# A sparse GNN and expert kernel on one core: one tile more gathered in quarter rows, the order of its gathers, and the queue of one weight load

## The chip, the cores and the metric

The kernel runs on one core of a Trainium2 chip. The metric is the device time of one execution in microseconds; the number to compare is the median over runs. Three runs of the kernel before gave 282.81, 284.5 and 288.1 us, so its median is 284.5 us.

## The reference

There are 625 rows of 1024 numbers. A first part (a relational graph layer over 20,000 edges) makes a new x; a second part adds a mixture of experts to it. The change lies in the second part, which is this:

```
xf = layernorm(x)                                   # 625 x 1024
sh = gelu(xf @ sW1[s] + sb1[s])                      # 2 shared experts, hidden 256
shared = mean over s of (sh @ sW2[s] + sb2[s])
gates = xf @ rW + rb;  w = softmax of the top 2 of 8 # per row
h = gelu(xf @ W1[e] + b1[e]);  y = h @ W2[e] + b2[e] # 8 experts, 1024 -> 256 -> 1024
out = x + shared + sum over e of w[e] * y[e]
```

All tensors are 32-bit floats. The kernel computes an expert only for the rows that chose it.

## The kernel before, in words

The first 119 us are the graph layer. Its last step writes the normalised rows to a DRAM tensor `h2d`, from which rows are gathered later. Then TensorE computes the first layer of the two shared experts (`p_sh`, line 1146, eight products of 128 by 512 in two column cuts for each of four blocks). In its shadow VectorE finds, for every row, the two best experts (`route`), and packs the rows into 11 tiles of 128 slots (`slots`): seven tiles (4 to 10) belong to one expert each, three (0, 1, 2) to two experts with 64 slots each, one (3) to four experts with 32 slots each. `tok` holds the row number of each slot of each tile. `quarter_rows` (line 1420) makes from it `tok4`: four row numbers for each slot, for a gather in which each partition gets quarters of four different rows, so that a transpose in blocks of 32 by 32 on VectorE gives the tile with columns on the partitions. For this TensorE multiplies four 128 by 128 selectors (`own4`, line 1424) with `tf`, a copy of `tok`, and VectorE scales the result into `tok4` (line 1431). `weights_T` (line 1400) splits the routing weights into three bfloat16 parts and transposes them; they are needed by the last products `p_o`.

`quarter_rows` is called from inside `shared_in(1, 0)`, between its two column cuts, by the argument `then` (line 1245). The instructions of each engine are put in order by the framework from the program's order and the waits written out as `tc.issue_after`.

Then comes the stage around the change, the first layer of the experts. It goes over the 11 tiles in the order

```
whole = range(NM2, NJ)
tiles = (*whole[:3], 0, whole[3], 1, whole[4], 2, *whole[5:], NH2)   # 4 5 6 0 7 1 8 2 9 10 3
by_quarters = [tiles[i] for i in (0, 1, 3, 5, 7, 9)]                 # 4 5 0 1 2 10
```

For each tile:

- `gather` (line 1465): GpSimd (POOL) issues indirect DMAs from `h2d` into the tile's rows `xs`, which have three buffers. A tile in `by_quarters` takes four, one for each quarter (line 1468); any other takes one of whole rows (line 1473).
- `fetch` (line 1477): a tile in `by_quarters` is turned by one VectorE transpose into `xsT` (line 1485). For any other, TensorE transposes the rows (`turn`, line 1496, two bursts `p_x` of four 128 by 128 transposes); ScalarE evicts the first burst (line 1502), VectorE the second (line 1500). The two first tiles are turned into the place of the second weights of expert 7 (`w2a[:, 7]`), which is free until those are loaded.
- `copy_w1` (line 1504): where a tile has several experts, ScalarE copies the weights of its second and further experts into `w1m` (line 1509).
- `expert_in` (line 1511): TensorE multiplies with the first weights (`p_h`, line 1515), VectorE copies the product to `hj` (line 1519), which has a single buffer, and SP's queue stores it in DRAM (`hd`, line 1521). Four more DMAs of SP's queue (`to_quarters`, line 1528) read the tile before this one back in another order as `hjT`.
- `expert_mid` (line 1534): VectorE transposes `hjT` in 32 by 32 blocks into `hT` (line 1537) and ScalarE applies bias and gelu (line 1542).

The second weights of experts 0 to 6 are loaded on SP's queue before the routing (`load_w2`, line 1182). Those of expert 7 are loaded on the same queue in step 2 of the loop over the tiles, when the products of tiles 4 and 5 have read what stood in their place.

Behind this stage TensorE computes the second layer (`p_yj`, line 1578), whose rows are scattered to DRAM (`yt`) and read back by row (`g`, line 1636), and the second layer of the shared experts (`p_o`, line 1676); VectorE adds all to x and the rows are stored.

Of the kernel before, what the change touches and what calls it, by code (L numbers as in the profile page):

```python
# [12 lines left out]
I32 = mybir.dt.int32  # L13
# [11 lines left out]
NE = 8  # L25
# [428 lines left out]
def sparse_kernel(  # L454
# [24 lines left out]
    nc = tc.nc  # L479

    def pool(stack, name, bufs=1, side="left", **kw):
        return stack.enter_context(tc.tile_pool(name=name, bufs=bufs, side=side,
                                                reuse_waits="tile", **kw))

    const = pool(ctx, "const")
# [10 lines left out]
    def ps_acc(name):  # L496
        return psum[0].tile([128, 512], F32, tag="acc", name=name, bufs=nacc[0])

    def ps_mm(name):
        return psum[0].tile([128, 512], F32, tag="mm", name=name, bufs=3)  # L500
# [146 lines left out]
    def bias_part(i):  # L647
        own = slice(0, (3 - i) * QC)
        near = b23.rearrange("p (k d) -> p k d", k=KD)
        if i:  # L650
# [14 lines left out]
                                    ap=[[0, 4], [D, QC], [1, D]]))  # L665
# [386 lines left out]
    turned = []  # L1052
# [90 lines left out]
    def shared_products(p, i, t, c, ks):  # L1143
        a, z = CUTS[c]
        for k in ks:
            nc.tensor.matmul(p[:, : z - a], sw1[:, i, k, t * 128 : (t + 1) * 128],  # L1146
                             h2T[:, k, a:z], start=(k == 0), stop=(k == KD - 1))
# [30 lines left out]
    io = pool(ctx, "io", 3)  # L1178
    w2a = pool(ctx, "w2a").tile([128, NE, HK, D], F32, name="w2a")

    def load_w2(e):
        nc.sync.dma_start(w2a[:, e], W2[e].rearrange("(k p) d -> p k d", p=128))

    for e in range(NE - 1):
        load_w2(e)
# [56 lines left out]

    shT = hid.tile([128, NS, HK, N], F32, name="shT")

    def shared_in(i, t, then=lambda: None):
        b = KD + i * HK + t
        for c, (a, z) in enumerate(CUTS):
            if a:
                then()
            first = not (i or t or c)  # L1250
            p = begun if first else ps_acc(f"p_sh_{i}_{t}_{a}")
            shared_products(p, i, t, c, range(AHEAD if first else 0, KD))
            nc.scalar.activation(shT[:, i, t, a:z], p[:, : z - a], AF.Gelu, bias=vT[:, b : b + 1])
# [5 lines left out]
    wab = const.tile([TP, 2, NT], F32, name="wab")  # L1259
    tok = const.tile([128, NJ], I32, name="tok")  # L1260
    tok4 = const.tile([128, 4, NJ], I32, name="tok4")
    quad = const.tile([128, 1], F32, name="quad")
    for b in range(4):
        nc.gpsimd.memset(quad[b * QC : (b + 1) * QC], float(b))
# [135 lines left out]
    def weights_T():  # L1400
        nc.vector.tensor_scalar(w[:, :, NS:], w[:, :, NS:], float(NS), None, op0=ALU.mult)
        NW_ = NS + NE
        part = rt.tile([TP, NT, 3 * QC], F32, name="part")
        nc.vector.memset(part, 0.0)
        near = const.tile([TP, NT, NW_], BF16, name="near")
        for i in range(3):
            nc.vector.tensor_copy(near, w)
            for j in range(3):
                at = j * QC + i * NW_
                nc.vector.tensor_copy(part[:, :, at : at + NW_], near)  # L1410
            if i < 2:
                nc.vector.tensor_sub(w, w, near)
        for a, b in ((0, 3), (3, NT)):
            p = ps_mm(f"p_wT_{a}")
            for d in range(a, b):
                nc.tensor.transpose(p[: 3 * QC, (d - a) * TP : (d - a + 1) * TP], part[:, d, :],
                                    ident[:TP, :TP])
            nc.vector.tensor_copy(wT[:, a * TP : b * TP], p[: 3 * QC, : (b - a) * TP])

    def quarter_rows():  # L1420
        own4 = rt.tile([128, 4, 4, QC], F16, tag="above", name="own4")
        tf = rt.tile([128, NJ], F16, name="tf")
        for a in range(4):
            nc.scalar.copy(own4[:, a], ident[:, None, a * QC : (a + 1) * QC].to_broadcast([128, 4, QC]))
        with tc.issue_after(named.ins):
            nc.vector.tensor_copy(tf, tok)
        q4 = ps_mm("p_tok4")
        for a in range(4):
            nc.tensor.matmul(q4[:, a * NJ : (a + 1) * NJ], own4[:, a].rearrange("p b r -> p (b r)"), tf,
                             start=True, stop=True)  # L1430
        return nc.vector.tensor_scalar(tok4.rearrange("p a j -> p (a j)"), q4[:, : 4 * NJ], 4.0, quad,
                                op0=ALU.mult, op1=ALU.add)

    gate()
    route()
    named = slots()
    weights_T()
    turned = []
    shared_in(1, 0, lambda: turned.append(quarter_rows()))
    shared_in(1, 1)  # L1440
    sh_in.close()

# [10 lines left out]
    def parts(j):  # L1453
        if j < NH2:
            return (0, HS, e_of[j]), (HS, 128, e_of[NH2 + j])
        if j < NM2:
            return [(QS * i, QS * (i + 1), e_of[nt + i]) for i in range(4)]
        return ((0, 128, e_of[NH2 + j - 1]),)

    xsT, w1m, copied, moved = {}, {}, [], []  # L1460
    acts = []
# [3 lines left out]
    def gather(j):  # L1465
        if j in by_quarters:
            for a in range(4):
                nc.gpsimd.indirect_dma_start(  # L1468
                    out=rows[j][:, a * (D // 4) : (a + 1) * (D // 4)], out_offset=None,
                    in_=h2d.rearrange("n (b f) -> (n b) f", b=4),  # L1470
                    in_offset=bass.IndirectOffsetOnAxis(ap=tok4[:, a, j : j + 1], axis=0))
        else:
            nc.gpsimd.indirect_dma_start(
                out=rows[j], out_offset=None, in_=h2d,
                in_offset=bass.IndirectOffsetOnAxis(ap=tok[:, j : j + 1], axis=0))
# [17 lines left out]
    def turn(j, g):  # L1493
        p = ps_acc(f"p_x{g}_{j}")
        for k in range(4):
            nc.tensor.transpose(p[:, k * 128 : (k + 1) * 128], half_row[j][:, 4 * g + k :: KD], ident)  # L1496
        o = xsT[j][:, 4 * g : 4 * g + 4, :]
        pv = p.rearrange("p (k n) -> p k n", k=4)
        if g:
            turned.append(nc.vector.tensor_copy(o, pv))  # L1500
        else:
            acts.append(nc.scalar.copy(o, pv))
# [8 lines left out]
    def expert_in(j):  # L1511
        p = ps_mm(f"p_h_{j}")
        for k in range(KD):
            for a, b, e in parts(j):
                nc.tensor.matmul(p[a:b, :H], xsT[j][:, k, a:b],  # L1515
                                 w1m[j, a][:, 0, k, :] if a else w1a[:, bass.ds(e, 1), k, :],
                                 start=(k == 0), stop=(k == KD - 1))
        h = xt.tile([128, H], F32, tag="hj", bufs=1, name=f"hj_{j}")
        copied.append(nc.vector.tensor_copy(h.rearrange("p (q c r) -> p c q r", q=4, c=HK),  # L1519
                                           p[:, :H].rearrange("p (c q r) -> p c q r", c=HK, q=4)))  # L1520
        moved.append(nc.sync.dma_start(hd[j], h))
        if j not in (tiles[0], tiles[-1]):
            with tc.issue_after(moved[-1].ins):
                to_quarters(tiles[tiles.index(j) - 1])

    def to_quarters(j):
        for q in range(4):
            nc.sync.dma_start(hjT[32 * q : 32 * q + 32, j].rearrange("t c (b r) -> t (c b r)", b=4)
                              .rearrange("t (b x) -> t b x", b=4),
                              hd[j].rearrange("(b t) (q x) -> q t b x", b=4, q=4)[q])  # L1530
# [15 lines left out]

    whole = range(NM2, NJ)
    tiles = (*whole[:3], 0, whole[3], 1, whole[4], 2, *whole[5:], NH2)
    by_quarters = [tiles[i] for i in (0, 1, 3, 5, 7, 9)]
    copies = {}  # L1550
    for i, (j, a, e) in zip((2, 3, 5, 6, 8, 9), ((j, a, e) for j in tiles for a, _, e in parts(j)[1:])):
        copies[tiles[i]] = [(j, a, e)]
    for i in (1, 0, 2):
        rows[tiles[i]] = io.tile([128, D], F32, tag="io", name=f"xs_{tiles[i]}")
    for i in (2, 0, 1):
        gather(tiles[i])
    for s in range(NJ + 2):
        if 0 < s <= NJ and tiles[s - 1] in half_row:
            turn(tiles[s - 1], 1)
        if s < NJ:  # L1560
            if s > 2:
                rows[tiles[s]] = io.tile([128, D], F32, tag="io", name=f"xs_{tiles[s]}")
                gather(tiles[s])
            fetch(tiles[s])
        if 0 <= s - 1 < NJ:
            expert_in(tiles[s - 1])
        if s == 2:
            load_w2(NE - 1)
        if 0 <= s - 4 < NJ - 3:
            expert_mid(tiles[s - 4])  # L1570
    ORDER = (*whole[:3], *range(NM2), *whole[3:])
# [38 lines left out]
    for n, j in enumerate(ORDER):  # L1610
        y = gat.tile([128, D], F32, tag="y", name=f"ys_{j}")
        for s in range(2):
# [3 lines left out]
            p = p_ys[j, s]  # L1616
# [47 lines left out]
    for d in range(NT):  # L1664
# [3 lines left out]
        for at in ((0, 512), (512, D)) if d < NT - 1 else ((0, 512), (512, 768), (768, D)):  # L1668
            n = at[1] - at[0]
            at = slice(*at)  # L1670
            p = (ps_mm if banks % 8 > 4 else ps_acc)(f"p_o_{d}_{at.start}")
# [21 lines left out]
def gnn_ffn_kernel(tc, *args):  # L1693
    nc = tc.nc
    with tc.tile_pool(name="flags", bufs=1) as flags:
        flag = flags.tile([1, 1], I32, name="flag")
        off = sparse_kernel(tc, flag, *args)
        with tc.If(off > 0):
            dense_kernel(tc, *args)
# [31 lines left out]
```

## Time and profile before

The profiled execution took 285.32 us, its span is 283.5 us, and the granted TensorE clock was 0.997 of full speed.

| | us | share of the span | instructions |
|---|---|---|---|
| TensorE matmul (PE) | 274.4 | 97% | 1509 |
| TensorE weight load (PEld) | 183.3 | 65% | 1509 |
| VectorE (DVE) | 175.7 | 62% | 446 |
| ScalarE (ACT) | 101.8 | 36% | 232 |
| GpSimd (POOL) | 61.1 | 22% | 122 |

The transfers sum to 64.48 MB, 227 GB/s over the span. SP's queue carries 48.74 MB of them, GpSimd's 15.04 MB, ScalarE's 0.35 MB.

How to read it: a line of a timeline is the start in us from the start of the span, the length, the engine, the line of the kernel, the operation, the tile that it writes and those it reads, and the number of instructions merged; in square brackets stands how long the engine was idle before it and what ended that. "SPq" is SP's queue of DMAs; the length is that of the issue, not of the transfer. Tile names are printed without their numbers. The chain that ended last is followed back from the last instruction: at each step to what released it, or to the instruction before it on its engine. Products are merged there, so that x16 is one tile's product with 128 slots (each 32-bit product counts as two instructions).

### The profile page before, as it was taken

The page shows a single profiled execution, that of the slowest core. Times are in us where ns is not written, and L with a number is a line of the kernel's source. Part 1 is how long each engine was busy: PE and PEld are TensorE (multiplying, and loading weights), DVE is VectorE, ACT ScalarE, POOL GpSimd, SP SyncE. Part 2 cuts the span into 40 slices and gives each one's busy share as a digit, 9 for nine tenths or more (in the row PEclk, how much of TensorE's full clock was granted, in tenths as well). Part 3 has the DMA queues.
Part 4 walks back from the last instruction along what each step waited for, and adds up shares of the span by engine and source line. Part 5 has one row for each costly group of instructions (what it writes and reads, how often), then busy time and mean ns, then how long its engine had stood idle before and what let it go on. Part 6 is the DMA issues. An engine that isn't in the chain of part 4 may idle for free.

```text
span 283.5 us, 4565 instructions
## 1 busy us (share of the span) xinstructions
PE 274.4 (97%) x1509; PEld 183.3 (65%) x1509; DVE 175.7 (62%) x446; ACT 101.8 (36%) x232; POOL 61.1 (22%) x122
## 2 busy tenths in 40 slices
PE   8899999999999999999999999799999999999993
PEld 7667777788888655677777787678544324444452
DVE  4889999999975689838930641555341312216972
ACT  2347326534642242445101150856298311100000
POOL 9810020000000032210047555360020222210000
PEclk9999999999999999999999999999999999999998
DMA  7999981000000899998999279754296554439962
GB/s 226 356 324 355 371 289 47 2 0 2 1 0 2 322 369 425 420 375 321 390 415 393 88 221 283 202 154 137 68 329 217 218 205 191 186 115 385 392 219 79
DMA packets 29987, 64.48 MB, mean 227 GB/s; under 512 B 8961, under 2 KB 16196, under 8 KB 28935
## 3 DMA queue, kind: packets, MB, share of 16 engines
q1 hardware_dynamic: 24475, 48.74, 47.9%
q0 software_dynamic: 5200, 15.04, 15.1%
q10 hardware_dynamic: 284, 0.35, 0.4%
q8 instruction: 14, 0.23, 0.3%
q14 instruction: 14, 0.11, 0.1%
HBM read 44.63 MB, written 20.26 MB: 229 GB/s over the span
## 4 chain that ended last, share of the span: by engine, by line
PE 82%; DMA 8%; DVE 7%; SPq 1%; issue 0%; ACT 0%; DVEq 0%
PE p_pr L956 15%; PE p_yj L1578 14%; PE p_o L1676 12%; PE p_sh L1146 12%; PE p_h L1515 10%; PE p_y L1031 6%; PE p_agg L985 5%; DMA xh<-in_x_dram 4%; DMA hd<-hj 4%; DVE st L777 2%; PE cnt L934 2%; PE p_t L844 2%; DVE ohs L903 1%; PE p_x L1496 1%; PE p_gate L1198 1%; PE p_y L1032 1%
## 5 line engine op out<-in xcount | busy, mean ns | idle before, releaser
L956 PE MATMUL p_pr<-wg,nT 128*125 128x286 f32 x240 | 62.4, 410 | 0.9 <-DVE neg L798 0.6
L956 PEld LDWEIGHTS p_pr<-wg,nT 128*125 128x125 f32 x240 | 43.3, 187 | 13.4 <-ACT nT L850 1.2
L1578 PE MATMUL p_yj<-w2a,hjT 128*128 (+2 forms) x88 | 38.7, 595 | 0.0
L1676 PE MATMUL p_o<-sw,shT 128*125 128x512 f32 (+1 forms) x88 | 36.3, 553 | 0.0
L1146 PE MATMUL p_sh<-h2T,sw 128*128 128x313 f32 (+1 forms) x128 | 35.3, 429 | 0.0
L1515 PE MATMUL p_h<-w1a,xsT 128*128 (+2 forms) x144 | 32.7, 380 | 1.5 <-DVE xsT L1485 1.5
L1578 PEld LDWEIGHTS p_yj<-w2a,hjT 128*128 128x128 f32 (+2 forms) x88 | 14.5, 168 | 23.3 <-issue 22.8
L1146 PEld LDWEIGHTS p_sh<-h2T,sw 128*128 128x128 f32 x128 | 23.6, 189 | 8.5 <-issue 0.2
L1515 PEld LDWEIGHTS p_h<-w1a,xsT 128*128 128x128 f32 (+2 forms) x144 | 22.8, 163 | 7.7 <-issue 1.7
L1676 PEld LDWEIGHTS p_o<-sw,shT 128*125 128x125 f32 x88 | 16.4, 187 | 16.9 <-issue 15.9
L1468 POOL DMA_INDIRECT xs<-h2d,tok x24 | 22.7, 946 | 19.0 <-issue 5.8
L1618 DVE COPY ys<-p_yj 128x512 f32<-128x512 f32 x15 | 10.3, 689 | 26.1 <-PE p_yj L1578 26.1
L1625 POOL DMA_INDIRECT yt<-ys,row x11 | 10.7, 970 | 48.9 <-DVE ys L1618 48.9
L1519 DVE COPY hj<-p_h 128x256 f32<-128x256 f32 x11 | 4.6, 421 | 24.5 <-PE p_h L1515 19.0
L1031 PE MATMUL p_y<-wo_t,eT 128*125 128x512 f32 (+1 forms) x40 | 18.8, 592 | 0.0
L1042 POOL DMA_DIRECT2D x1d<-xh x4 | 2.2, 542 | 65.6 <-DVE flagf L727 62.1
L1542 ACT ACTIVATE hjT<-hT,vT 128x128 f32<-128x128 f32 (+2 forms) x34 | 9.8, 354 | 17.1 <-DVE hT L1537 10.2
L985 PE MATMUL p_agg<-P,CT 125*125 125x288 f32 x100 | 15.5, 305 | 0.0
L1515 PE MATMUL p_h<-w1m,xsT 128*64 128x256 f32 (+1 forms) x96 | 14.7, 381 | 0.0
L1647 DVE SCALAR_TENSOR_TENSOR x<-g,wab,x 125x1024 f32<-125x1024 f32 (+1 forms) x12 | 13.2, 1105 | 1.9 <-DMA g<-yt 1.7
L1578 PE MATMUL p_yj<-w2m,hjT 128*64 128x512 f32 (+1 forms) x48 | 14.1, 595 | 0.0
L904 DVE TENSOR_TENSOR ohs<-ohs,cols 125x1024 f16<-125x1024 f16 (+1 forms) x22 | 14.0, 638 | 0.0
(306 smaller groups left out, 415.7 us busy)
## 6 DMA issues: line engine op xcount, KB each, us to landing
w1a<-in_L_ffn_W_dram SPq DMA_DIRECT2D x8, 1024.0 KB
w2a<-in_L_ffn_W_dram SPq DMA_DIRECT2D x8, 1024.0 KB
yt<-zero SPq DMA_DIRECT2D x2, 2560.0 KB
g<-yt SPq DMA_DIRECT2D x10, 512.0 KB
sw<-in_L_ffn_sW_dram SPq DMA_DIRECT2D x4, 1024.0 KB
h2d<-h POOLq DMA_DIRECT2D x5, 448.0 KB, 9.5
out_dram<-x SPq DMA_DIRECT2D x4, 448.0 KB
x<-x1d SPq DMA_DIRECT2D x1, 1500.0 KB
```

The source lines that it names most:

```text
L904: last = nc.vector.tensor_tensor(os, os, both(VV_, 128)[1], op=ALU.mult)
L956: product = nc.tensor.matmul(p[:TP, :F], nT[:, k, m * TP : (m + 1) * TP], wg[:, k, r, :], start=(k == 0), stop=(k == KD - 1))
L985: nc.tensor.matmul(p[:TP, : F + 2], CT[:, m, at : at + TP], P[:, m, r, i], start=(m == 0 and i == 0), stop=(m == NT - 1 and i == 1))
L1031: nc.tensor.matmul(ps[s][:TP, :], eT[:n, k, :], wo_t[:n, k, at], start=(k == 0), stop=False)
L1146: nc.tensor.matmul(p[:, : z - a], sw1[:, i, k, t * 128 : (t + 1) * 128], h2T[:, k, a:z], start=(k == 0), stop=(k == KD - 1))
L1468: nc.gpsimd.indirect_dma_start(out=rows[j][:, a * (D // 4) : (a + 1) * (D // 4)], out_offset=None, in_=h2d.rearrange("n (b f) -> (n b) f", ...
L1515: nc.tensor.matmul(p[a:b, :H], xsT[j][:, k, a:b], w1m[j, a][:, 0, k, :] if a else w1a[:, bass.ds(e, 1), k, :], start=(k == 0), stop=(k == ...
L1578: made = nc.tensor.matmul(p[a:b], hjT[:, j, k, a:b], (w2m[j, a, k] if a else w2a[:, bass.ds(e, 1), k])[..., s * 512 : (s + 1) * 512], star ...
L1618: copied.append(nc.vector.tensor_copy(y[:, at], p))
L1625: sent.append(nc.gpsimd.indirect_dma_start(out=yt, out_offset=bass.IndirectOffsetOnAxis(ap=row[:, j : j + 1], axis=0), in_=y, in_offset=No ...
L1647: added.append(nc.vector.scalar_tensor_tensor(*args, op0=ALU.mult, op1=ALU.add))
L1676: nc.tensor.matmul(p[:TP, :n], shT[:, i, k, own], sw2[:, i, k, at], start=(i == 0 and k == 0), stop=False)
```

## The change

Five edits belong together:

1. `quarter_rows` is called right after `slots`, ahead of `weights_T`, and no longer from inside `shared_in`.
2. The tiles in quarter rows are those at places 0, 1, 3, 4, 6, 8 and 10 of the order (4, 5, 0, 7, 8, 9, 3) in place of 0, 1, 3, 5, 7 and 9 (4, 5, 0, 1, 2, 10). TensorE turns 6, 1, 2 and 10 in place of 6, 7, 8, 9 and 3.
3. Four tiles, not three, have their rows allotted and their gathers issued ahead of the loop. On POOL's own list of instructions the gathers of the fourth tile (0) keep their place, their buffer and their wait.
4. The fifth tile (7) takes its four row numbers from `tok5`, a copy of 128 by 4 numbers that VectorE makes right behind the copy of tile 4's product.
5. The second weights of expert 7 are loaded by ScalarE's queue. On ScalarE's list the load stands behind six copies of `w1m` and ahead of two more.

```diff
-    def load_w2(e):
-        nc.sync.dma_start(w2a[:, e], W2[e].rearrange("(k p) d -> p k d", p=128))
+    def load_w2(e, eng=nc.sync):
+        eng.dma_start(w2a[:, e], W2[e].rearrange("(k p) d -> p k d", p=128))
...
-    def shared_in(i, t, then=lambda: None):
+    def shared_in(i, t):
...
-            if a:
-                then()
...
+    tok5 = const.tile([128, 4], I32, name="tok5")
...
     named = slots()
+    turned = [quarter_rows()]
     weights_T()
-    turned = []
-    shared_in(1, 0, lambda: turned.append(quarter_rows()))
+    shared_in(1, 0)
     shared_in(1, 1)
...
-                    in_offset=bass.IndirectOffsetOnAxis(ap=tok4[:, a, j : j + 1], axis=0))
+                    in_offset=bass.IndirectOffsetOnAxis(
+                        ap=tok5[:, a : a + 1] if j == tiles[4] else tok4[:, a, j : j + 1], axis=0))
...
+        if j == tiles[0]:
+            with tc.issue_after(copied[-1].ins):
+                nc.vector.tensor_copy(tok5, tok4[:, :, tiles[4]])
         moved.append(nc.sync.dma_start(hd[j], h))
...
-    by_quarters = [tiles[i] for i in (0, 1, 3, 5, 7, 9)]
+    by_quarters = [tiles[i] for i in (0, 1, 3, 4, 6, 8, 10)]
...
-    for i in (1, 0, 2):
+    for i in (1, 0, 2, 3):
         rows[tiles[i]] = io.tile([128, D], F32, tag="io", name=f"xs_{tiles[i]}")
-    for i in (2, 0, 1):
+    for i in (2, 0, 1, 3):
         gather(tiles[i])
...
-            if s > 2:
+            if s > 3:
...
         if s == 2:
-            load_w2(NE - 1)
+            with tc.issue_after(acts[-1].ins):
+                load_w2(NE - 1, nc.scalar)
```

## The prediction

> **What bounds the kernel now.** I read the page first (busy shares), then the chain that ended last, then busy time by stretch, then the timelines of the stretch that the change touches (145 to 205 us).
>
> ```profile
> span 283.5 us, 4565 instructions
> ...
> PE   8899999999999999999999999799999999999993
> ```
>
> TensorE is busy nearly throughout; one slice outside the first and last is a 7. The table of busy time by stretch says how little idle there is (columns: stretch, its length, then busy us of each engine, clock, DMA share, GB/s):
>
> ```profile
> 166.00:180.00 14.00, 12.49 (x82) 9.98 (x81) 7.08 (x9) 3.96 (x9) 8.51 (x9) 1.00 0.87 258
> 180.00:204.00 24.00, 24.00 (x197) 18.51 (x198) 10.18 (x18) 13.12 (x33) 5.67 (x6) 1.00 0.49 141
> 204.00:248.00 44.00, 44.00 (x151) 17.36 (x151) 11.72 (x20) 19.60 (x35) 9.71 (x10) 1.00 0.59 218
> ```
>
> From 32 us to the last product near 279 us TensorE idles only in 166 to 180, for 14.00 - 12.49 = 1.51 us. So inside the touched part the end moves only through (a) TensorE work removed, (b) that hole, (c) new holes. The chain shows what made the hole (start, length, what):
>
> ```profile
> 166.00 0.44 DVE hj L1519
> 166.46 6.23 DMA hd<-hj
> 172.81 0.44 DVE hj L1519
> 173.26 3.74 DMA hd<-hj
> 177.25 0.09 issue
> 177.46 0.42 DVE hT L1537
> 177.87 1.95 DVE xsT L1485
> 179.82 0.14 issue
> 179.95 3.67 PE p_h L1515 x32
> 183.63 0.64 PE p_x L1496 x4
> 184.27 3.46 PE p_h L1515 x16
> 187.73 0.44 PE p_x L1496 x4
> 188.17 3.60 PE p_h L1515 x32
> ```
>
> The tile hj has one buffer, so VectorE may not copy the next tile's product until the DMA of the last one to DRAM (hd) has landed. VectorE is in order: the transpose xsT of tile 1 stands behind two such copies and ends at 179.8; TensorE, free at 178.4, starts at 179.95. The first of those DMAs took 6.23 us, the second 3.74. Just ahead of the slow one on SP's queue stands one megabyte of second weights (w2a, expert 7); the timeline of SP's queue:
>
> ```profile
> 162.55 0.35 SPq L1521 DMA_DIRECT2D hd<-hj  x1
> 165.99 0.38 SPq L1182 DMA_DIRECT2D w2a<-in_L_ffn_W_dram  x1
> 166.46 0.42 SPq L1521 DMA_DIRECT2D hd<-hj  x1
> ```
>
> **The change, part by part.** Tiles run in the order 4, 5, 6, 0, 7, 1, 8, 2, 9, 10, 3. Before, TensorE turns 6, 7, 8, 9, 3; after, 6, 1, 2, 10. All other tiles are gathered in quarter rows and turned by VectorE.
>
> *One tile less turned by TensorE.* It loses two bursts of four transposes. In the chain a burst takes 0.44 us after a whole tile and 0.64 after a tile of two halves; three bursts still follow such a tile, so the two lost are the cheap ones: 2 x 0.44 = 0.88 us, on the path. ScalarE loses one eviction (0.59), VectorE one (0.69) and gains one transpose (2.03): +1.34 us for VectorE, in a stretch (166 to 180) where it is busy 7.08 of 14. POOL goes from 6 x 4 + 5 = 29 gathers to 7 x 4 + 4 = 32: three more at 0.95 + 0.30 = 1.25 us, 3.75 us of issue. POOL is busy 8.51 of those 14 us, and its last gather before starts at 189.55, for a tile turned from 199.4 on: covered there, provided that the gathers near 170 are in time (below).
>
> *quarter_rows ahead of weights_T.* The same instructions. In the changed order TensorE makes the row numbers after three products of the shared expert instead of after eight and the wT transposes. From 140.70 at 2.74/5 = 0.55 us a product that is 142.3; the input tf is ready at 141.76 and own4 at 130.8, so no wait. VectorE's tok4 ends near 143 instead of 146.0; the last three copies of part (0.43 us) slip behind it to about 143.5, and TensorE reaches wT at 142.6 + 2 x 0.55 = 143.7: nothing. POOL can start the eight quarter gathers at 143.8, behind the whole-row gather that ends at 143.49, not at 146.28. DMA share is 1.02 or more until 156 (seven weight loads), so their data come at most 2.5 us sooner, and TensorE is in p_sh until 158.37 anyhow: worth nothing on the path. It lets the gathers of tile 0 begin near 156 instead of 158.54.
>
> *Fourth gather emitted ahead.* Tile 0's gathers stand in the same place in POOL's order, wait for the same buffer and the same transpose: nothing.
>
> *Fifth held back.* tok5 is a 128x4 copy on VectorE right behind hj of tile 4; the nearest row, a 128x11 cast, takes 0.17 us, and VectorE then waits 3.47 us anyhow. Tile 7's gathers cannot start before 162.52 + 0.17 + 0.30, about 163.0; a whole-row gather of tile 7 started at 163.54 before. Now there are four, to 163.0 + 4 x 1.25 - 0.3 = 167.7, and behind them on POOL the whole rows of tile 1 (167.9 to 168.9; 166.67 to 171.4 before, in quarters), then tile 8. TensorE needs them as follows. Tile 6's product starts at 166.24, tile 0's near 169.70 and ends near 173.30; tile 1's first burst is then due, and tile 7's product at 173.94. VectorE needs 2.03 + 0.14 for tile 7's transpose, so its rows must have landed, and VectorE be free, by 171.8. Gathers take 2.7/3.3/7.8 us to land (minimum, median, maximum of the trace): from 167.7 that is 170.4, 171.0 or 175.5; tile 1's rows, from 168.9, at 171.6, 172.2 or 176.7, against 173.30. At the median both are in time; at the maximum the holes are 3.7 and 3.4 us (they overlap). I take the median, since the 7.8 belongs with the weight loads at full DMA share, and keep 3.7 for the range.
>
> *Expert 7's second weights on ScalarE's queue.* Both orders want tile 5's product done (166.0). On ScalarE the issue stands behind six w1m copies, 163.03 + 6 x 0.53 = 166.2, so it waits for nothing; at 0.38 us like SP's it delays only the two w1m copies behind it, used at 177.8, and the next eviction (173.9). SP loses the issue and its 3 us of waiting. What matters is the landing of tile 5's hd, issued at 166.45 as before, beside the megabyte instead of behind it. Bounds: 6.23 us if sharing the engines is as bad as queueing, 3.74 (the next hd; the one of 162.55 needed at most 3.45) if it is as if alone. I take 4.2, near the low end, because hd moves an eighth of the bytes. Then hj of tile 6 starts at 170.7 and ends at 171.1, and tile 7's transpose is done at 173.1: no hole. At 6.23 it ends at 175.3 and the hole is 1.5 again. Further on: hj of tile 0 must wait for the hd issued at 171.2 and hj of tile 7 for that of tile 0. At 3.74 each, hj of tile 7 starts at 179.1, and the eviction of tile 1's second burst behind it ends at 180.6, while TensorE wants it at the middle of tile 1's product, 177.84 + 1.8 = 179.6: a hole of 1.0. At 2.2 (the hd of 177.55 let hj go at 179.73) there is none. I take 0.3.
>
> [...]
>
> **Sum.** -0.88 (transposes) - 1.51 (hole) + 0.3 (what is left of it) = -2.1 us. Behind 180 TensorE has no gap in which this could be lost (24.00 of 24.00 and 44.00 of 44.00 us, then its products up to 278.8 in the chain): the sw2 loads, scatters and stores hang on its products and shift with it. Against the profiled execution (285.32 us, span 283.5) that is 283.2; the median of the three, 284.5, lies 0.8 lower, so 282.4.
>
> **Rivals.**
> *The hole only moves* (tile 1's rows late, or hd still slow): for it, DMA share is 1.06 to 1.11 at 170 to 174, where the new gathers land; against it, median landings. Hole of 1.0 to 2.0: gain 0.4 to 1.4, time 283.1 to 284.1.
> *Slower: the held-back fifth is late.* Four gathers instead of one behind tok5, with 1 MB of weights beside them; tile 7's transpose waits, TensorE behind it. The place is the turn of tile 7 at 171.8; it decides from a hole over 0.88 + 1.51 = 2.4 us, rows landing after 174.2, 6.5 us from the last issue at 167.7. At 7.8 the hole is 3.7, net +1.3: 285.8.
> *The cover of VectorE goes too*: the last quarter tile (3) is turned near 195.5 to 197.5 against a product due at 198: with an hd or gather 2 us late there, another 1.5 us, so 286 to 287.
> *More than the hole*: only a start of tile 4's product before the end of p_sh could give it, and p_sh is TensorE's own work; excluded but for noise.
>
> **Chances.** Forecast (gain 1.5 to 2.4: 282.1 to 283.0) 0.55; the hole moves (283.1 to 284.1) 0.28; even or slower (to 287) 0.12; more 0.05. Three runs before spread from 282.81 to 288.1, so about 2% (5.7 us) is what a measurement can tell. The range goes from the forecast's low end less 1.7 and a little (the lowest run's distance to the median), 280.0, to the slow rival's 285.8 and a little, 286.5. The likeliest case alone: 281 to 284. Below 278.8 needs more than all of TensorE's idle in the part: 0.03. Above 290.2 needs several holes: 0.04. Within 2%: 0.93.
>
> **What would show it.** Right: tile 5's hd lands within 4.7 us; TensorE's busy time falls by about 0.9 and shows 32 transposes on it instead of 40; hole under 0.5 us between 166 and 182; the first p_yj starts near 201.7 instead of 203.8; first quarter gather near 143.8. Wrong: TensorE waiting for tile 7's transpose or for tile 1's rows, hj still waiting 3 us or more on hd, or a gap behind 180.

## The result, and the profile after

On the first occasion the changed kernel took 287.62 us (median of 22 runs, 284.65 to 290.78) against 284.62 us (22 runs, 282.79 to 289.01) for the kernel before: a ratio of 1.0081, 95% interval 1.0052 to 1.0109. A ratio leaves out executions more than 1.5 per cent above the fastest of the same kernel, so it is not the quotient of the two medians. The changed kernel is slower by 0.8 per cent where a gain was forecast: 282.4 was expected, and 287.62 lies above the range's upper end of 286.5. The interval speaks of one occasion only, so I measured the unedited changed kernel on four more; that is part of the experiments and changes how this figure is to be read.

The page of the changed kernel's profiled execution (288.9 us, span 287.1):

```profile
span 287.1 us, 4563 instructions
...
PE   8999999999999999999999996979999999999993
```

The single 7 of before has become a 6 and, two slices on, another 7. Busy time by stretch of the same execution (columns as in the prediction):

```profile
166.00:180.00 14.00, 11.14 (x62) 7.46 (x61) 5.64 (x6) 3.25 (x7) 6.59 (x7) 1.00 0.70 218
180.00:204.00 24.00, 22.48 (x152) 17.18 (x154) 11.90 (x18) 12.82 (x31) 8.50 (x9) 1.00 0.52 147
204.00:248.00 44.00, 44.00 (x203) 17.86 (x196) 11.59 (x21) 19.70 (x36) 8.75 (x9) 1.00 0.59 213
```

TensorE idles 14.00 - 11.14 = 2.86 us in the first stretch (before 1.51) and 1.52 us in the second (before nothing).

One measure makes all profiles comparable. TensorE's groups give the start of the first expert product and of the first second product; first the kernel before, then the changed one (last columns: first and last start):

```profile
L1515 PE MATMUL p_h<-w1a,w2a x32: 379/379/454, 158.4 to 165.6; 128*128 x32
...
L1578 PE MATMUL p_yj<-w2a,hjT x88: 592/592/697, 203.7 to 247.0; 128*128 x56, 128*64 x24, 128*32 x8
```

```profile
L1515 PE MATMUL p_h<-w1a,w2a x32: 379/379/382, 157.9 to 165.1; 128*128 x32
...
L1582 PE MATMUL p_yj<-w2a,hjT x88: 592/592/697, 207.1 to 250.4; 128*128 x56, 128*64 x24, 128*32 x8
```

I call the time between the two starts *the stage*: 45.36 us before, 49.14 after (by the trace's nanoseconds). In every profile of this study the time from the first second product to the last product on TensorE is the same 74.81 us, and the part ahead of the stage varies from 156.0 to 160.0 us whatever the kernel. So the stage holds whatever the change does, and one profile's span alone says little: the five profiles of the changed kernel differ by up to 2.2 us ahead of the stage.

What stopped TensorE in this execution is not what the prediction named. VectorE's copies of tiles 6 and 1 wait for "remote", which is a release that the profile cannot put down to anything, and ScalarE's eviction for tile 2 waits for nothing visible, until the same moment (timelines of VectorE and of ScalarE):

```profile
165.49 0.42 DVE L1519 COPY hj<-p_h 128x256 f32<-128x256 f32 x1 [3.39 <-PE p_h L1515]
...
175.37 0.42 DVE L1519 COPY hj<-p_h 128x256 f32<-128x256 f32 x1 [6.80 <-remote]
...
189.52 0.42 DVE L1519 COPY hj<-p_h 128x256 f32<-128x256 f32 x1 [4.58 <-remote]
```

```profile
189.62 0.58 ACT L1502 COPY xsT<-p_x 128x512 f32<-128x512 f32 x1 [4.43 <-issue]
```

TensorE, in the middle of tile 0's product, creeps at one instruction per 0.72 us (its timeline; "issue" means that it waited for nothing the profile shows):

```profile
173.16 0.38 PE L1515 MATMUL p_h<-w1a,xsT 128*64 x1 [1.01 <-issue]
173.88 0.42 PE L1515 MATMUL p_h<-w1m,xsT 128*64 128x256 f32 x1 [0.34 <-issue]
174.60 0.42 PE L1515 MATMUL p_h<-w1m,xsT 128*64 128x256 f32 x1 [0.31 <-issue]
175.29 0.43 PE L1515 MATMUL p_h<-w1a,xsT 128*64 x1 [0.27 <-issue]
```

Products that creep count as busy (0.38 to 0.43 us of each 0.72): the stage is 3.78 us longer, though TensorE idles only 2.87 us more in it (4.38 against 1.51) and has eight transposes less to do.

The trace's semaphore events fit that. VectorE's wait for tile 5's hd is over at 172.09, 6.15 us after the issue; then it waits for the event of TensorE's product of tile 6, which ended at 169.35 and whose event comes at 175.35. That of tile 1 (185.62) comes at 189.50. The trace also holds only 2336 events of DMA landings, where that of the kernel before holds 3045. So the first thing to find out was whether this belongs to the kernel.

### The profile page after: what moved, and what is told of

Same layout as the page of the kernel before. It is cut to its first block, busy times and chain, and to the rows that moved or that the text cites. A ratio compares the mean times of both kernels' runs of the same rounds, so it can differ in the third digit from the quotient of the medians.

```text
span 287.1 us, 4563 instructions
## 1 busy us (share of the span) xinstructions
PE 275.7 (96%) x1501; PEld 182.4 (64%) x1501; DVE 176.8 (62%) x447; ACT 101.8 (35%) x231; POOL 63.5 (22%) x125
## 4 chain that ended last, share of the span: by engine, by line
PE 79%; DVE 8%; DMA 4%; another core or an unknown queue 3%; issue 3%; SPq 1%; ACT 0%; DVEq 0%
PE p_pr L956 15%; PE p_yj L1582 13%; PE p_o L1680 12%; PE p_sh L1146 12%; PE p_h L1515 8%; PE p_y L1031 6%; PE p_agg L985 5%; DMA xh<-in_x_dram 4%; DVE xsT L1485 2%; DVE st L777 2%; PE cnt L934 2%; PE p_t L844 2%; DVE ohs L903 1%; PE p_gate L1198 1%
## 5 line engine op out<-in xcount | busy, mean ns | idle before, releaser
L1515 PE MATMUL p_h<-w1a,xsT 128*128 (+2 forms) x144 | 33.5, 382 | 3.7 <-DVE hj L1519 1.4
L1467 POOL DMA_INDIRECT xs<-h2d,tok x28 | 26.5, 945 | 17.5 <-issue 7.5
L1515 PE MATMUL p_h<-w1m,xsT 128*64 128x256 f32 (+1 forms) x96 | 15.5, 383 | 0.6 <-issue 0.6
```

The costliest lines, as they stand in the source:

```text
L1467: nc.gpsimd.indirect_dma_start(out=rows[j][:, a * (D // 4) : (a + 1) * (D // 4)], out_offset=None, in_=h2d.rearrange("n (b f) -> (n b) f", ...
L1515: nc.tensor.matmul(p[a:b, :H], xsT[j][:, k, a:b], w1m[j, a][:, 0, k, :] if a else w1a[:, bass.ds(e, 1), k, :], start=(k == 0), stop=(k == ...
```

## The experiments

All ratios are to the kernel before, run beside each on the same occasion.

**The changed kernel again, four times, and the kernel before, twice; nothing edited.**

> The changed kernel once more, nothing edited: a second profile. If its two long waits (VectorE's copy of tile 6 at 9.4 us behind the hd's issue and of tile 1 at 7.5 us, both released together with ScalarE or TensorE) belong to the kernel, they come again at the same two tiles, and the time is 286 to 288.5 us. If they belong to that one profiled execution, they are gone or elsewhere, while the time stays 286 to 288.5 and another wait shows.

> The changed kernel a third time, nothing edited. The first measurement gave 1.0081 of before, the second 0.9958. If the kernel itself is slower, 1.005 or more again; if the first belongs to its occasion, 0.993 to 1.000, no semaphore event of TensorE over 1 us late, and from the first expert product to the first second product 44.5 to 45.5 us (44.87 in the second, 49.14 in the first).

> The kernel before, nothing edited, with a second profile. Ratio 0.997 to 1.003. From the first expert product to the first second product 45 to 46.5 us (45.36 in its first profile), with one hole of TensorE of 1 to 2 us before tile 1.

> The changed kernel a fourth time, nothing edited. If the first measurement (1.0081) was of its occasion: 0.992 to 1.000 of before, and 44.5 to 45.5 us from the first expert product to the first second product. If the kernel has two kinds of occasion in equal parts: 1.005 or more, with semaphore events of TensorE and VectorE several us behind the instructions that make them.

> The changed kernel, nothing edited, a fifth time. Either 0.993 to 0.999 of before with 44.5 to 45.5 us from the first expert product to the first second product, and semaphore events on time; or 1.005 to 1.012 with 49 to 50 us and events up to 7 us late. Nothing between.

> The kernel before, nothing edited, on the same occasion. If late events belong to the occasion, it has them whenever the changed kernel beside it has; its ratio stays 0.997 to 1.003 and its stage 45 to 46.5 us if they cost it nothing, as they cost the pieces with the old set nothing.

| unedited | ratio (95% interval) | stage, us | tile 6's copy behind tile 5's hd, us |
|---|---|---|---|
| changed, first | 1.0081 (1.0052 to 1.0109) | 49.14 | 9.43 |
| changed, second | 0.9958 (0.9931 to 0.9985) | 44.87 | 5.97 |
| changed, third | 0.9958 (0.9927 to 0.999) | 45.12 | 6.25 |
| changed, fourth | 1.0105 (1.0068 to 1.0142) | 49.80 | 9.41 |
| changed, fifth | 0.995 (0.9922 to 0.9979) | 45.07 | 6.19 |
| before, first profile | | 45.36 | 6.35 |
| before, second | 0.9993 (0.9954 to 1.0032) | 45.76 | 6.67 |
| before, third | 0.9999 (0.9958 to 1.0041) | 48.03 | 7.66 |

(The last column is the start of tile 6's copy less the start of the issue of tile 5's hd, in the trace.) The changed kernel has two kinds of occasion and nothing between, as expected of the fifth: on three it gains 0.42 to 0.50 per cent, about 1.2 to 1.4 us; on two it loses 0.8 to 1.05. The fourth repeats the first to the detail, at the same tiles (timeline of VectorE in the fourth):

```profile
173.89 0.42 DVE L1519 COPY hj<-p_h 128x256 f32<-128x256 f32 x1 [6.78 <-remote]
...
188.59 0.42 DVE L1519 COPY hj<-p_h 128x256 f32<-128x256 f32 x1 [4.58 <-remote]
```

The third and the fourth ran on the same chip, so it isn't the chip. The other three show the kernel itself. The chain of waits of the third, where the prediction showed 6.23 and 3.74 for before:

```profile
165.92 6.12 DMA hd<-hj
172.17 0.44 DVE hj L1519
172.62 2.91 DMA hd<-hj
```

Beside the megabyte, on another queue, tile 5's hd takes 6.12 us (6.07 in the chain of the fifth). The trace's records of single DMA pieces show what it waits for. From 166.8 to 170.1 us these are all the queues that moved anything (view of the DMA queues; columns: packets, that is single pieces, MB, and the share of the 16 engines' time):

```profile
q10 hardware_dynamic: 227, 0.93, 81.8%
q0 software_dynamic: 32, 0.07, 6.1%
```

q10 is ScalarE's queue, and 227 of the load's 256 pieces of 4 KB go in this stretch; q0 is that of the gathers, which nearly stop; q1, SP's queue with hd, moves nothing. Its first piece of hd starts at 170.16, 4.2 us after the issue. So both hd and the gathers came late because the engines were at the megabyte. In the kernel before it is the same with the load on SP's queue: from 167.2 to 170.8 us that queue moved 1.02 MB, no piece of hd among it, and the gathers 0.01 MB.

Two waits of TensorE follow (its timeline in the third):

```profile
174.07 0.71 PE L1496 MATMUL p_x<-ident,xs 128*128 128x128 f32 x4 [1.13 <-DMA xs<-h2d,tok]
...
181.44 0.43 PE L1515 MATMUL p_h<-w1a,xsT 128*64 x1 [0.77 <-DVE xsT L1500]
```

The first is for tile 1's rows, the second for the eviction of tile 1's second burst behind the copy of tile 7. They make 1.90 us; the hole of before was 1.51. Tile 1's rows took 6.65 us from issue to landing (6.49 in the second profile, 6.40 in the fifth). The hole moved.

**The load alone on ScalarE's queue.**

```diff
...
-            load_w2(NE - 1)
+            with tc.issue_after(acts[-1].ins):
+                load_w2(NE - 1, nc.scalar)
```

> The kernel before, with one edit: the second weights of expert 7 go out on ScalarE's queue. Theory A (this load does the harm: the hd of tile 5 does not pass the megabyte on another queue and VectorE's copy of tile 6 comes later still): 286 to 288 us, copy of tile 6 more than 6.5 us behind that hd's issue. Theory B (the harm comes from the new set of tiles, with longer runs of gathers on POOL): 283 to 284.6 us, and the copy of tile 6 at most 6.2 us behind the issue. The prediction's own step says 283.0 to 283.3, with the copy 4.2 us behind the issue.

1.0016 (0.998 to 1.0053), stage 48.69. No gain; neither theory's number is met cleanly. The copy comes 5.7 us behind the hd's issue, not 4.2. Here the hd was not held back until the load was through: from 167.5 to 170 us pieces of both queues go side by side (view of the DMA queues), and it landed after 5.60 us all the same:

```profile
q10 hardware_dynamic: 205, 0.83, 87.1%
q1 hardware_dynamic: 105, 0.10, 11.6%
```

The edit also changed the scheduler's order on VectorE: tile 7's second-half eviction now stands behind the copy of tile 0, which waits for tile 6's hd (5.07 us, with the megabyte all but through and gathers beside it). TensorE waits 2.96 us for that eviction, its longest single wait in the study. That is a cost which the diff doesn't show.

**All but that: the changed kernel with the load back on SP's queue.**

```diff
...
-            with tc.issue_after(acts[-1].ins):
-                load_w2(NE - 1, nc.scalar)
+            load_w2(NE - 1)
```

> The changed kernel with the second weights of expert 7 back on SP's queue. Theory A (the load on ScalarE's queue does the harm): 283.5 to 285 us, both holes of the changed kernel (near 172 to 175 and 190 to 193.6) gone or under 1.5 us. Theory B (the new set of tiles): 287 to 288 us, holes as in the changed kernel.

0.998 (0.9941 to 1.002). It lies within 0.3 per cent of the three good occasions of the changed kernel: the queue makes no difference that can be told. The expectation of theory A is met by the time, but not by the waits of its one profile, which shows the longest of the twelve executions (288.64 us): the stage is 46.96 us there, tile 6's copy comes 8.38 us behind the hd's issue, and TensorE waits up to 2.01 us. I don't set that profile beside the others. Here too VectorE's order changed (tile 7's transpose ahead of tile 6's copy).

**The early row numbers alone.**

```diff
...
-    weights_T()
-    turned = []
-    shared_in(1, 0, lambda: turned.append(quarter_rows()))
+    turned = [quarter_rows()]
+    weights_T()
+    shared_in(1, 0)
```

> The kernel before, with only the quarter rows' numbers made ahead of the transposed weights. Prediction's step: nothing, 284.2 to 285.0. Theory C (the earlier gathers bring a later, fuller stretch and do the harm by themselves): 286 us or more.

> The kernel before, with the row numbers made early and the load of expert 7's second weights issued six tiles later on SP's queue; tiles as before. Theory D: the hd behind it lands in 4 us or less, the hole before tile 1 closes, 0.5 to 1.5 us under the kernel with early rows alone (which was at 0.9946 of before), so 0.989 to 0.993 of before. If the load never mattered: 0.993 to 0.997.

0.9946 (0.991 to 0.9981), stage 44.84. The second kernel was meant to move the load as well, but the scheduler put it back in its place on SP's queue and the order of every engine's work is that of the first: it is a second measurement of the early rows, 0.9925 (0.9893 to 0.9958), stage 43.71. So this edit, costed at nothing in the prediction, is worth 0.5 to 0.75 per cent. What moved is the gathers: tile 7's whole rows go out at 159.64, 3.2 us after the first expert product, instead of 163.54, 5.2 us after. Tile 5's hd then needs 4.67 us in the chain instead of 6.23, while that of tile 4, now beside that gather, needs 4.06. Part of the 4.67 is only where the count starts: tile 4's late hd puts off tile 5's, so the load goes out 1.19 us ahead of it instead of 0.47. From the load's issue to the landing of hd it is 5.86 us, before 6.70.

**The changed kernel with the old set of six tiles.**

```diff
-    by_quarters = [tiles[i] for i in (0, 1, 3, 4, 6, 8, 10)]
+    by_quarters = [tiles[i] for i in (0, 1, 3, 5, 7, 9)]
```

> The changed kernel with the set of quarter-row tiles of the kernel before (six: 4, 5, 0, 1, 2, 3); the fourth gather ahead, the early row numbers and the weights on ScalarE's queue stay. Theory A (the load): 286 to 288 us. Theory B (the set): 283 to 285 us.

(The six tiles are 4, 5, 0, 1, 2 and 10; the expectation has 3 for the last.) 0.9923 (0.9887 to 0.9958), theory B's side, with one profile whose stage (46.05, a hole of 1.97) does not fit it. Taken alone it is inconclusive; the clean comparison of the sets is the one in pieces below.

**The load in the same queue, six tiles later.**

```diff
-        if s == 2:
+        if s == 8:
             with tc.issue_after(acts[-1].ins):
                 load_w2(NE - 1, nc.scalar)
```

> The changed kernel with the same load of expert 7's second weights on the same ScalarE queue, but issued six tiles later, behind the runs of gathers near 166 to 174 us; VectorE's order stays as in the changed kernel. Theory D (the megabyte shares the 16 engines with the hd of tile 5 and the quarter rows of tiles 7 and 8, and each comes late): 283 to 285 us, hd of tile 5 landed within 4 us, no hole of TensorE over 1 us before 182. Theory B (the longer runs of gathers alone): 286.5 to 288, hd still 5 us or more.

0.992 (0.9894 to 0.9946), stage 45.32. VectorE's order is that of the changed kernel, so only the load moves. Busy time by stretch, and then the end of the stage in the chain of waits:

```profile
166.00:180.00 14.00, 14.00 (x98) 10.48 (x98) 8.62 (x10) 6.22 (x14) 8.36 (x10) 1.00 0.70 210
180.00:204.00 24.00, 21.82 (x169) 16.21 (x166) 9.72 (x16) 9.76 (x26) 6.43 (x7) 1.00 0.57 164
```

```profile
185.18 3.63 PE p_h L1515 x32
189.06 0.12 issue
189.17 0.11 DVE hT L1540
189.28 6.39 DMA hd<-hj
...
197.20 2.01 PE p_h L1515 x8
```

Without the megabyte the first hole is gone. With it, issued at 186.72, the hd of 189.28 takes 6.39 us and opens a hole of 2.15 us there instead. With the load in its old place, the hd of the same tile (2) had landed after 2.15 us in the kernel before (issued at 192.28) and 1.81 in the third profile of the changed kernel (192.03), by the trace's semaphore events. Tile 1's rows land after 5.19 us instead of 6.40 to 6.65. The delay goes with the load in both places (6.12 us for tile 5's hd in the third profile, 6.39 for tile 2's here). That decides for theory D. The megabyte is not the only thing that delays an hd: beside gathers, with the megabyte issued only 0.62 us ahead of the landing or all but through, 4 to 5 us were seen as well (4.06 and 5.07 above).

**Tile 7's gathers not held back.**

```diff
-                    in_offset=bass.IndirectOffsetOnAxis(
-                        ap=tok5[:, a : a + 1] if j == tiles[4] else tok4[:, a, j : j + 1], axis=0))
+                    in_offset=bass.IndirectOffsetOnAxis(ap=tok4[:, a, j : j + 1], axis=0))
...
-        if j == tiles[0]:
-            with tc.issue_after(copied[-1].ins):
-                nc.vector.tensor_copy(tok5, tok4[:, :, tiles[4]])
```

> The changed kernel without the small copy that holds back tile 7's gathers: they follow tile 0's at once, some 1.4 us sooner, while the load stays on ScalarE's queue. Theory E (the held-back fifth is late): 1.0 to 1.5 us under the changed kernel, 285.5 to 286.5. Theory D (the megabyte): within 0.5 us of the changed kernel.

0.9935 (0.9903 to 0.9966), stage 44.31: 0.56 to 0.81 us under the three good profiles of the changed kernel, and in its median 1.38 us under the one beside it (282.71 against 284.09). TensorE's wait for tile 1's rows falls from 0.95 to 0.17. Theory E holds as a second, smaller cause; with the load in pieces (below) nothing is left of it.

**The load in four pieces.**

```diff
-        if s == 2:
+        if s in (2, 4, 6, 8):
+            k, half = (s - 2) // 4, slice((s // 2 + 1) % 2 * 512, (s // 2 + 1) % 2 * 512 + 512)
             with tc.issue_after(acts[-1].ins):
-                load_w2(NE - 1, nc.scalar)
+                nc.scalar.dma_start(w2a[:, NE - 1, k, half], W2[NE - 1][k * 128 : (k + 1) * 128, half])
```

> The changed kernel with expert 7's second weights in four DMAs of 256 KB on ScalarE's queue, two tiles apart, in place of one of a megabyte. Theory D (a hd waits for the bytes put into the engines beside it, whatever the queue): hd never over 5 us, no hole of TensorE over 0.7 us, 43.0 to 44.0 us from the first expert product to the first second product, 0.989 to 0.993 of before. If the weights don't matter: as the changed kernel, 44.5 us or more.

> The changed kernel with the load in four pieces, a second time: 0.985 to 0.991 of before and 42.8 us from the first expert product to the first second product, whether the changed kernel beside it is of the quick or of the long kind, if the long waits need the megabyte beside the gathers; 47 us or more on an occasion of the long kind if they need the gathers alone.

> As the last, and without the copy that holds back tile 7's gathers. Theories D and E together: 42.8 to 43.6 us from the first expert product to the first second product (the kernel with early rows alone needed 43.71 without a hole, and this has eight transposes fewer, 0.88), 0.987 to 0.992 of before.

> The changed kernel with expert 7's second weights in four pieces, and with the old set of six quarter-row tiles. If the set is worth its eight transposes (0.88 us) once the hd is quick: 43.6 to 44.0 us from the first expert product to the first second product, against 42.80 with the seven tiles, and 0.3 per cent more time than those pieces. If the order of VectorE that comes with the old set (the eviction of tile 7's second half behind the copy of tile 0) costs a hole as well: 44.5 us or more.

> The kernel before with one edit: expert 7's second weights in four pieces of 256 KB on ScalarE's queue. If the load is the whole matter: 43.6 to 44.2 us from the first expert product to the first second product, no hole of TensorE over 0.5 us, and 0.989 to 0.993 of before. If the early row numbers are needed as well (without them the rows of tile 0 and 7 come 2 us later beside tile 5's hd): 44.5 us or more and 0.994 or more.

| four pieces, with | ratio (95% interval) | stage, us |
|---|---|---|
| the changed kernel | 0.9874 (0.9826 to 0.9922) | 42.80 |
| the changed kernel, a second time | 0.9878 (0.9833 to 0.9923) | 42.80 |
| the same, fifth not held back | 0.9883 (0.9837 to 0.993) | 42.80 |
| the old set of six tiles | 0.9915 (0.9885 to 0.9946) | 43.68 |
| the kernel before, nothing else | 0.9918 (0.9879 to 0.9958) | 45.08 |

The first is the best kernel of the study: 281.56 us against 284.98 for before. Its stretches, and when the pieces go and tile 6's copy starts (timelines of ScalarE's queue and of VectorE):

```profile
166.00:180.00 14.00, 14.00 (x101) 10.35 (x99) 8.31 (x9) 6.13 (x14) 8.35 (x10) 1.00 0.76 219
180.00:204.00 24.00, 24.00 (x174) 16.94 (x171) 10.69 (x18) 12.34 (x31) 6.10 (x7) 1.00 0.58 164
```

```profile
162.81 0.36 ACTq L1573 DMA_DIRECT2D w2a<-in_L_ffn_W_dram  x1
163.65 0.35 ACTq L1573 DMA_DIRECT2D w2a<-in_L_ffn_W_dram  x1
...
178.95 0.33 ACTq L1573 DMA_DIRECT2D w2a<-in_L_ffn_W_dram  x1
...
186.11 0.33 ACTq L1573 DMA_DIRECT2D w2a<-in_L_ffn_W_dram  x1
```

```profile
168.69 0.42 DVE L1519 COPY hj<-p_h 128x256 f32<-128x256 f32 x1 [0.87 <-PE p_h L1515]
```

Tile 6's copy waits for its product now, not for the hd (issued at 165.19). Two things changed at once: the pieces are small, and the first two go out ahead of that hd, since that half of the weights' place is free as soon as tile 4's product is done. Which of the two counts more was not taken apart; but in the profiles of the old set and of the kernel before with pieces only one piece goes out ahead of that hd, and tile 6's copy comes 3.44 us behind its issue all the same. With no hole left the sets can be compared: 43.68 - 42.80 = 0.88 us for the eight transposes. The last row of the table is undecided: by its ratio the load is the whole matter, by its stage (waits of 0.59 and 0.17 us are left) the early rows are needed as well. The second measurement of the early rows adds to that: its stage of 43.71 us has no hole, with the megabyte where it stood.

The pieces with the old set ran on the occasion of the fourth measurement. Only three of the twenty profiles lack landing events: the changed kernel's first (2336) and fourth (2361) and this one (2347), against 3045 to 3152 in all others. So something marks the occasion, not the kernel. But this one lost nothing by it: no hole, 43.68 us. The long waits came with the megabyte beside the gathers, in two of five profiles of the changed kernel, and in none of the six profiles with the load moved or cut, only one of which is of such an occasion. What marks the occasion, whether the recording itself has a part in it, and why events of TensorE come late there, stays open.

## Why the prediction was wrong

*The step that failed* is "I take 4.2, near the low end, because hd moves an eighth of the bytes". Tile 5's hd took 6.12 and 6.07 us in the chains, practically the upper bound of 6.23 that stood for "sharing the engines is as bad as queueing". The prediction itself says what follows: "At 6.23 it ends at 175.3 and the hole is 1.5 again". A second term failed for the same reason: the new gathers were given the median landing of 3.3 us, and tile 1's rows took 6.40 to 6.65. The profile before had a sign of it: its four gathers issued beside the megabyte (166.67 to 170.42) have a median of 5.3 us.

The 4.2 was my estimate between the bounds of 3.74 and 6.23, and no run shows it with the megabyte on ScalarE's queue. In the third profile no piece of hd moved from 166.8 to 170.1 us, while 227 of the load's 256 went; with the load alone on ScalarE's queue pieces of both queues went side by side (205 and 105 from 167.5 to 170 us). Tile 5's hd landed 6.12 us after its issue in the first case and 5.60 in the second; the shortest with the load there is that of the old set of tiles, where tile 6's copy starts 5.05 us behind the issue.

These two terms account for 1.3 to 1.6 of the 5.2 us between 282.4 and 287.62. The other 4 us or so are those of the first occasion (below), and what caused them is not known.

*Minus 0.88 for the transposes*: right, 0.88 (43.68 to 42.80).

*Minus 1.51 for the hole, plus 0.3*: wrong. 1.64 and 1.90 us of waits are there in the second and third profile, so the net is +0.1 to +0.4 instead of -1.2. The place of the second (tile 1's second burst behind tile 7's copy) was named, and mis-sized: 0.3 taken, 0.69 to 0.77 measured, 1.0 as the bound.

*Tile 1's rows in time at the median*: wrong by 0.86 to 1.13 us. The rival "the hole only moves" (283.1 to 284.1, chance 0.28) is what happens on three of five occasions, for the two reasons it gives: it named a gain of 0.4 to 1.4 us, and the ratios give 1.2 to 1.4 (medians 284.09, 284.21 and 283.86). That the gain came so near is partly luck, since the next two terms, both put at nothing, pull in opposite directions.

*Early row numbers worth nothing*: wrong, 0.5 to 0.75 per cent alone. The chains fit an effect through the overlap of the gathers with hd, where the prediction looked at TensorE's inputs alone; no run takes that apart.

*Holding back the fifth, nothing*: wrong by 0.56 to 0.81 us of the stage, as long as the megabyte goes beside it.

*The first measurement's extra 4 us of stage* were foreseen by no rival: it is neither rival's mechanism, and its cause stays open. The late-fifth rival gave 285.8 and a hole of 3.7; that magnitude came, but VectorE waited for no rows.

*Nothing lost behind 180*: wrong on its terms; the wait for the eviction of tile 1's second burst (0.69 to 0.77 us) stands there, or just ahead of it, in the good profiles.

## What to carry to other kernels

Where a small DMA is on the path, ask which bytes are put into the engines just ahead of it and beside it, on whatever queue (6.23 us for 128 KB behind a megabyte on the same queue, 6.12 beside it on another), and move or cut those; another queue alone bought nothing here (1.0016). After an edit, compare the order of every engine, since a scheduler may move an eviction behind a wait that the diff doesn't touch. Measure a change of under one per cent on more than one occasion, and compare the time of the touched stage between two anchors instead of the span.

## What the runs showed that was not expected

A hole of 2.49 us cost twice. In the third profile of the kernel before, tile 5's hd takes 7.54 us and TensorE idles 2.49 us; then its granted clock is 0.50 from 180.5 to 183.9 us and the product takes 5.36 us for what took 3.67 in the prediction's chain, 1.69 us more (busy by stretch, then chain):

```profile
176.80:179.30 2.50, 0.01 (x2) 0.04 (x2) 2.50 (x4) 2.03 (x5) 0.94 (x1) 1.00 0.58 180
180.50:183.90 3.40, 3.40 (x20) 2.42 (x18) 0.00 (x0) 2.67 (x7) 0.00 (x0) 0.50 0.68 216
```

```profile
164.81 7.54 DMA hd<-hj
...
179.29 5.36 PE p_h L1515 x32
```

The same came after the hole of 2.96 us with the load alone on ScalarE's queue (0.50 from 178.8 to 182.2 us), and not after the 2.15 us with the load six tiles later, where the clock stays at 1.00 (194.5 to 204 us). It also came in the fourth profile of the changed kernel (0.50 from 174.1 to 177.5 us), behind creeping products with several waits of at most 1.03 us, and not in the first, which creeps as well with waits of at most 1.01 us (1.00 from 166 to 180 us). What decides it was not shown.

The mean granted clock of each execution gives an estimate of how often: it is 0.991 in the third profile of the kernel before and in that of the load alone on ScalarE's queue, both with such a stretch, 0.994 in the fourth of the changed kernel, and 0.997 in the first profile of before, which has none in the stage. On the six later occasions 34 of 140 executions of the kernel before have 0.991 or less, with a median of 286.9 us against 285.0 for the others. With the load alone on ScalarE's queue it is 6 of 12; in the changed kernel on its three good occasions none of 36. So part of its gain there is that it has no execution with so low a mean clock: with those of the kernel before left out, its gain by the means is 0.9 to 1.1 us instead of 1.1 to 1.6.
